# One set of expert blocks in place of two in a fused graph, attention and expert layer: 114 blocks, seven slots apart among the gathers

## The chip, the cores and the metric

The kernel runs on one core of a Trainium2 chip. The metric is the time of one execution on the device in microseconds (us), the median of several runs. The core has five engines with a queue of instructions each: PE (matmuls, with its weight loads shown as PEld), DVE (vector work, reads PSUM), ACT (activations and copies), POOL (here almost only indirect DMAs, which gather or scatter rows by a list of indices) and SP (issues the plain DMAs). Each queue runs in order and waits on semaphores for the others. Transfers between memory (HBM) and the on-chip SBUF run on 16 DMA engines.

## The reference

6250 nodes with 256 features, 100,000 edges, 16 experts, two experts a node:

```python
xn = layernorm(x)
# graph part, dinv = rsqrt(segment_sum(edge_weight, dst) + 1)
h   = xn @ W
agg = segment_sum((dinv[src] * edge_weight * dinv[dst])[:, None] * h[src], dst) + (dinv * dinv)[:, None] * h
g   = relu(0.5 * (layernorm(agg + b) * gamma + beta) + 0.5 * xn)
# linear attention, 8 heads of 32
q, k = elu(xn @ Wq.T) + 1, elu(xn @ Wk.T) + 1;  v = xn @ Wv.T
m   = ((q @ (k.T @ v)) / max(q @ k.sum(), 1e-6)) @ Wproj.T + bproj
x   = x + g + m
# experts
y   = layernorm(x)
top2, idx = top_k(y @ gate_w + gate_b, 2);  w = softmax(top2)
moe = sum over k of w[k] * (relu(y @ w1[idx[k]] + b1[idx[k]]) @ w2[idx[k]] + b2[idx[k]])
out = x + layernorm(y + moe) * f_gamma + f_beta
```

## The kernel before

Nodes lie in 49 tiles of 128 rows (the last has 106); `X` holds all of x in SBUF. Edges come sorted by destination, so each chunk of 128 edges adds into a window of two tiles. `gps_layer` tests this and takes `windowed_layer`. After the node degrees and the first norms, a loop over *slots* does everything that is left. A slot from 0 to 781 handles one chunk of 128 edges: POOL gathers the 128 source rows from `hs` (L1155), DVE builds the weighted one-hot matrix `hot` (L1159), and six slots later (`LAG`) PE multiplies both into the accumulator `acc` (L1168), which DVE adds into the tile's aggregate (L1177). All other work is woven in between: `weave.add(slot, piece)` registers a Python generator, the loop runs every piece that is due at a slot up to its next `yield n`, and puts it back n slots later. A slot is thus a place in the order of every engine's queue, not a time; PE, DVE, ACT and SP keep this order as it is written (`by_hand`). The slots go on behind 781, without gathers, until nothing is left.

The pieces that matter here:

- `residual(ts_)` finishes two tiles (graph norm, attention, relu), writes the new x and the gate's logits.
- `route(...)` runs for a *phase*, a group of tiles. It takes the top two experts of each token and gives each pair a row in `xslots`, a tensor in HBM of blocks of 128 rows, each block of one expert. An expert's last, part-filled block stays open (`fill`, `had`, `open`) and takes tokens of the next phase. Full blocks are put in a list in the order in which they become full (`queue` counts them, `code` holds them), and `listed` writes expert and block number of entries lo to hi into `rows`. Where `flush` is set, open blocks are closed too. `usual` goes to zero when a phase's list is shorter than the plan in the code needs (or longer, for a flush); then a second loop behind the first one runs every possible block and every combine once more.
- `scatter(...)` normalises the phase's tiles and POOL scatters their rows to `xslots` (L911), two DMAs a tile.
- `expert(...)` runs block j of the list. At its slot SP reads two registers from `rows`, asks for the first half of the expert's weights (512 KB) and for the block's 128 rows; 5 slots later for the second half (642 KB); at +9 PE transposes the rows (`xtp`, L973), at +11 it makes the hidden layer (`hp`, L983), at +13 the output (`yp`, L992), to which DVE adds the bias (L996); at +15 SP stores 128 rows to `yslots`. For the first blocks the steps are one slot shorter twice. Four weight buffers take turns.
- `token_weights` makes the two softmax weights; `combine(ts_)` gathers for two tiles their two rows each from `yslots` (POOL, L1019), adds them with the weights (DVE, L1030), normalises and writes `out`.

The blocks are in two sets with tensors, lists and states of their own: tiles 0 to 35 in eight phases, tiles 36 to 48 in three. Each set ends with a flush.

```python
SETS = ((8, 12, 16, 20, 24, 28, 32, 36), (42, 46, NT))
USUAL = [2 * CUT + 11, 2 * (NT - CUT) + 12]        # 83 and 38 blocks are run
hi = USUAL[z] if flush else max(0, 2 * (b - CUT * z) - 11)
block = max(block + (4 if z else 8 if n < 3 else 5 if flush else 6), ready)
```

So blocks start every 8, 6 and 5 slots in the first set and every 4 in the second, and not before their phase's routing is ready. Combines of tiles 0 to 35 may start 18 slots after the start of the first set's last block, those of the other tiles 18 slots after the start of the last block. One combine (two tiles) starts every 5 slots, and none before the last `residual` is 24 slots old. `fill` writes zeros into `xslots` and `yslots` ahead of their use, a megabyte at a time.

Of the kernel before, what the change touches and what calls it, by code (L numbers as in the profile page):

```python
# [117 lines left out]
SETS = ((8, 12, 16, 20, 24, 28, 32, 36), (42, 46, NT))  # L118
CUT = SETS[0][-1]
USUAL = [2 * CUT + 11, 2 * (NT - CUT) + 12]  # L120
MOST = [(2 * n + NE * (P - 1)) // P for n in (CUT * P, N - CUT * P)]

# [114 lines left out]
def windowed_layer(ctx: ExitStack, tc: tile.TileContext, X, rows3, ident, loc_t, w_t, W, b, gamma, beta, wqT, wkvT, wprojT, bproj,  # L237
# [12 lines left out]
    xslots = [dram.tile([(m + 1) * P, D], F32, name=f"w_xslots{i}") for i, m in enumerate(MOST)]  # L250
    yslots = [dram.tile([(m + 1) * P, D], F32, name=f"w_yslots{i}") for i, m in enumerate(MOST)]
# [110 lines left out]
    def fill(z, a):  # L362

        zero = zero_b.bitcast(F32)
        for s in range(0, MOST[z] + 1, 8):
            q = min(8, MOST[z] + 1 - s)
            nc.sync.dma_start(a[s * P:(s + q) * P, :].rearrange("(p q) c -> p q c", q=q),
                              zero[:, None, :].to_broadcast([P, q, D]))
            yield 8

    for _ in fill(0, xslots[0]):
        pass
# [350 lines left out]

    states = [state(f"s{z}") for z in range(len(SETS))]

# [27 lines left out]
    def listed(s, ps_row, lo, hi, most, closed):  # L753


        code = mp.tile([1, P], I32, name="code_i", bufs=1)[:, lo:hi]
        v.tensor_tensor(code, ps_row[0:1, lo:hi], iota_row[0:1, lo:hi], op=OP.add)
        v.tensor_scalar(s["rows"][:, 1, lo:hi], code, 8, None, op0=OP.logical_shift_right)
        v.tensor_scalar(s["rows"][:, 1, lo:hi], s["rows"][:, 1, lo:hi], float(NE - 1), float(P), op0=OP.min, op1=OP.mult)
        v.tensor_scalar(code, code, 255, None, op0=OP.bitwise_and)  # L760
        if not closed:
            past = small("past", P)[0:1, lo:hi]
            v.tensor_scalar(past, iota_row[0:1, lo:hi], s["queue"][0:1, :], 256.0, op0=OP.is_ge, op1=OP.mult)
            v.tensor_tensor(code, code, past, op=OP.add)
        v.tensor_scalar(s["rows"][:, 0, lo:hi], code, float(most), float(P), op0=OP.min, op1=OP.mult)

    def route(z, a, b, lo, hi, fresh, flush):
# [3 lines left out]
        s = states[z]  # L771
# [40 lines left out]
        if flush:  # L812
            done = small("done")
            v.tensor_copy(done, new)
        if not fresh:
# [60 lines left out]
        if hi > lo:  # L876
            row = bank("row")
            nc.tensor.matmul(row[0:1, :P], s["code"], ident, start=True, stop=True)
            listed(s, row, lo, hi, MOST[z], flush)
        v.scalar_tensor_tensor(usual, s["queue"][0:1, :], float(hi), usual,  # L880
                               op0=OP.is_le if flush else OP.is_ge, op1=OP.mult)

        if not flush:
            yield 1
            v.tensor_copy(s["last"], d[:, NE * m:])
# [7 lines left out]
    def scatter(z, n, a, b, ahead, kind, each):  # L893
# [13 lines left out]
        for t in range(a, b):  # L907
            r = rows(t)
            y = places[t]()
            for k in range(2):  # L910
                i = nc.gpsimd.indirect_dma_start(  # L911
                    out=xslots[z], out_offset=IndirectOffsetOnAxis(ap=slot_i[:r, t, k:k + 1], axis=0),
                    in_=y[:r], in_offset=None).ins
                for m in range(n + 1):
                    tc.declare_no_dep(i, group=f"tokens{z}_{m}", reason="every token has slots of its own")
                tc.declare_no_dep(i, group=f"loads{z}", reason="blocks that are read are full")
                tc.add_to_no_dep_group(f"tokens{z}_{n}", i)
# [24 lines left out]
    def expert(z, n, j, homes, bank, gap):  # L942

        def row(i):
            if not loaded.get((z, i)):
                _, regs = nc.values_load_multi_w_load_instructions(
                    states[z]["rows"][0:1, i, j:min(j // 8 * 8 + 8, ends[z, j])], engines=[mybir.EngineType.SP],
                    min_val=0, max_val=(MOST[z] if i == 0 else NE - 1) * P,
                    skip_runtime_bounds_check_because="bounded by a minimum where it is computed")
                loaded[z, i] = list(regs)  # L950
            return loaded[z, i].pop(0)
# [7 lines left out]
        i = sync(xs, xslots[z][bass.ds(slots, P), :])  # L959
        if n is not None:  # L960
            for m in range(n + 1, len(SETS[z])):
                tc.declare_no_dep(i, group=f"tokens{z}_{m}", reason="a full block takes no more tokens")
            tc.add_to_no_dep_group(f"loads{z}", i)
# [36 lines left out]
        i = sync(yslots[z][bass.ds(slots, P), :], y)  # L1000
        if n is not None:
            tc.declare_no_dep(i, group=f"stores{z}", reason="every block has rows of its own", keep=[before_it])
            tc.add_to_no_dep_group(f"stores{z}", i)
        homes["y"].give(y_)

    def combine(ts_, homes, pool, last):
# [7 lines left out]
        for i, t in enumerate(ts_):  # L1014
            r = rows(t)
            z = 0 if t < CUT else 1
            for k in range(2):
                got[i, k] = homes["got"].take()
                nc.gpsimd.indirect_dma_start(  # L1019
                    out=got[i, k]()[:r], out_offset=None, in_=yslots[z],  # L1020
                    in_offset=IndirectOffsetOnAxis(ap=slot_i[:r, t, k:k + 1], axis=0))
# [68 lines left out]
    to_fill = [(0, yslots[0]), (1, xslots[1]), (1, yslots[1])]  # L1090
    fill_at = 4
    for z, a in to_fill:
        weave.add(fill_at, fill(z, a))
        fill_at += 8 * ((MOST[z] + 8) // 8)
# [6 lines left out]
    a = 0  # L1101
    for z, phases in enumerate(SETS):
        lo = 0
        for n, b in enumerate(phases):
            flush = n == len(phases) - 1
            for t0 in range(a, b, 2):
                t1 = min(b, t0 + 2)
                at = max(at, min(NCH, 16 * t1 + 4) + LAG + 3)
                weave.add(at, residual(range(t0, t1)))
                last_at = at  # L1110
                for t in range(t0, t1):
                    summed_at[t] = at + 3
                    if t + RING < NT and t >= 4:
                        sum_from(t + RING)
                at += 10
            hi = USUAL[z] if flush else max(0, 2 * (b - CUT * z) - 11)
            ready = max(last_at + RES, scattered - 2)
            weave.add(ready, route(z, a, b, lo, hi, n == 0, flush))
            if flush:
                weave.add(ready + 6, token_weights(CUT * z, b))  # L1120
            slow = 0 if z and flush else 1
            weave.add(ready + 2, scatter(z, n, a, b, 9, "token" if slow else "got", slow))
            scattered = ready + 11 + 2 * (b - a) * slow
            ready += 14 + (2 * (b - a) * slow)
            for j in range(lo, hi):
                ends[z, j] = hi
                block = max(block + (4 if z else 8 if n < 3 else 5 if flush else 6), ready)
                weave.add(block, expert(z, n, j, homes, bank, (4, 3) if n < 3 and z == 0 else (5, 4)))
            lo, a = hi, b
        if z == 0:  # L1130
            ready_a = block + 18
# [56 lines left out]
    with tc.If(again), ExitStack() as tail:  # L1188
# [16 lines left out]
        for z, s in enumerate(states):  # L1205
            row = bank("row")
            nc.tensor.matmul(row[0:1, :P], s["code"], ident, start=True, stop=True)
            listed(s, row, 0, MOST[z], MOST[z], True)
            for j in range(MOST[z]):
                ends[z, j] = MOST[z]  # L1210
                weave.add(block, expert(z, None, j, homes, bank, (5, 4)))
                block += 4
# [493 lines left out]
```

## Time and profile before

| | |
|---|---|
| runs | 1540.73, 1544.71, 1543.6 us; median 1543.6 |
| profiled execution | 1551.48 us, of which the span shown is 1549.6 |
| busy share of the span | PE 83%, PEld 66%, DVE 59%, ACT 34%, POOL 62% |
| mean granted PE clock | 0.932 |
| DMA | 367.43 MB, mean 237 GB/s |
| chain that ended last | PE 41%, DVE 16%, DMA 12%, issue 10%, ACT 3% |
| expert blocks | 121 transfers each of `xslots` blocks, `yslots` blocks and both weight halves |

The page shows one profiled execution, which took some 8 us longer than the median run. The busy share is a mean over stages that have different limits. In a row of a group, the columns are line, engine, operation, out<-in and count, then busy time and mean ns of one, then the engine's idle time just before these instructions and what ended most of it. In order of time, a row is start, duration, engine, line, operation and, in brackets, the idle time before it and what ended it.

### The profile page before, as it was taken

What the parts mean: (1) busy time and instruction counts of PE and PEld (TensorE: products, weight loads), DVE (VectorE), ACT (ScalarE), POOL (GpSimd) and SP (SyncE); (2) the same over time, 40 slices, a digit from 0 to 9 for tenths busy, and PEclk for the clock granted to TensorE, in tenths of its full rate; (3) what the DMA queues carried; (4) which work ended last, traced back from release to release, by engine and by line L of the source; (5) the groups of instructions that cost most, each with busy time, mean ns of one, the idle gap of its engine ahead of it and who ended that gap; (6) DMA issues with size and microseconds to landing.
All of it is one profiled execution on the core that took longest, in us unless ns stands there. A gap on an engine that the chain in (4) does not pass through costs nothing.

```text
span 1549.6 us, 24825 instructions
## 1 busy us (share of the span) xinstructions
PE 1282.6 (83%) x7112; PEld 1017.6 (66%) x7112; DVE 918.8 (59%) x3246; ACT 519.5 (34%) x1388; POOL 965.7 (62%) x999
## 2 busy tenths in 40 slices
PE   4879999989767989898999989889999987777820
PEld 3836666666545767677787778768877865666620
DVE  7754444468855755646465475754573737788045
ACT  3654444423221323223232323323332334344220
POOL 1027777777777777777777777777677545551042
PEclk9999999999878999999999989989999999799975
DMA  9789933333345766768887868678888866999832
GB/s 288 250 288 378 356 104 99 99 99 117 101 166 182 230 219 233 238 221 276 277 281 259 278 234 295 210 237 301 316 292 301 299 245 225 327 360 326 313 95 68
DMA packets 180847, 367.43 MB, mean 237 GB/s; under 512 B 27091, under 2 KB 118152, under 8 KB 180694
## 3 DMA queue, kind: packets, MB, share of 16 engines
q1 hardware_dynamic: 132746, 236.69, 43.9%
q0 software_dynamic: 47712, 128.17, 25.9%
q8 instruction: 63, 1.03, 0.3%
q10 hardware_dynamic: 236, 0.80, 0.2%
q14 instruction: 90, 0.74, 0.2%
HBM read 290.00 MB, written 75.54 MB: 236 GB/s over the span
## 4 chain that ended last, share of the span: by engine, by line
PE 41%; DVE 16%; DMA 12%; issue 10%; ACT 3%; POOL 1%; SPq 0%; ACTq 0%; POOLq 0%; DVEq 0%
PE acc L1168 12%; PE yp L992 9%; DMA rows<-w_hs,src_t 8%; PE hp L983 8%; PE hp L667 3%; PE mix L683 2%; DMA early<-in_experts 2%; DVE hot L1159 2%; PE kq L549 2%; DMA w_xslots<-Q,slot_i 1%; DVE xn L1030 1%; DVE bnst L312 1%; DVE agg L1177 1%; PE tp L638 1%; PE gl L710 1%
## 5 line engine op out<-in xcount | busy, mean ns | idle before, releaser
L1155 POOL DMA_INDIRECT rows<-w_hs,src_t x782 | 758.1, 969 | 335.5 <-issue 91.1
L1168 PE MATMUL acc<-rows,hot 128*128 128x256 f32 x1564 | 447.3, 399 | 59.0 <-DMA rows<-w_hs,src_t 48.9
L1168 PEld LDWEIGHTS acc<-rows,hot 128*128 128x128 f32 x1564 | 276.9, 196 | 125.3 <-issue 51.1
L1159 DVE TENSOR_SCALAR hot<-iota_g,loc_t,w_t 128x128 f32<-128x128 f32 x782 | 244.9, 352 | 6.0 <-PE acc L1168 5.4
L1019 POOL DMA_INDIRECT Q<-w_yslots,slot_i x98 | 99.4, 1015 | 167.0 <-issue 90.2
L992 PE MATMUL yp<-early,hT 128*128 128x256 f32 x592 | 152.1, 403 | 24.0 <-ACT hT L988 24.0
L983 PE MATMUL hp<-Q,early 128*128 128x128 f32 x1184 | 150.4, 282 | 10.1 <-ACT Q L977 10.1
L983 PEld LDWEIGHTS hp<-Q,early 128*128 128x128 f32 x1184 | 146.5, 197 | 17.9 <-ACT Q L977 14.5
L992 PEld LDWEIGHTS yp<-early,hT 128*128 128x128 f32 x592 | 116.9, 201 | 46.2 <-ACT hT L988 29.3
L988 ACT ACTIVATE hT<-hp,early 128x128 f32<-128x128 f32 x296 | 84.3, 367 | 178.2 <-PE hp L983 108.1
L911 POOL DMA_INDIRECT w_xslots<-Q,slot_i x98 | 102.3, 1044 | 43.1 <-issue 32.0
L977 ACT COPY Q<-xtp 128x256 f32<-128x256 f32 x121 | 44.8, 370 | 232.6 <-PE xtp L973 226.2
L1177 DVE SCALAR_TENSOR_TENSOR agg<-acc,dinv,agg 64x256 f32<-64x256 f32 x135 | 65.1, 482 | 94.4 <-PE acc L1168 91.9
L983 PE MATMUL hp<-Q 128*128 128x128 f32 x752 | 101.1, 292 | 12.8 <-ACT Q L977 12.7
L983 PEld LDWEIGHTS hp<-Q 128*128 128x128 f32 x752 | 96.7, 205 | 20.1 <-ACT Q L977 18.7
L996 DVE TENSOR_TENSOR Q<-yp,early 128x256 f32<-128x256 f32 x74 | 31.2, 422 | 125.6 <-PE yp L992 124.4
L992 PE MATMUL yp<-Q,hT 128*128 128x256 f32 x376 | 92.8, 390 | 9.6 <-ACT hT L988 9.6
L549 PE MATMUL kq<-early,xnT 128*128 128x512 f32 (+1 forms) x196 | 96.6, 616 | 4.4 <-ACT xnT L545 4.4
L555 DVE SCALAR_TENSOR_TENSOR row<-two_a,two_b 128x256 f32<-128x256 f32 (+1 forms) x49 | 21.0, 429 | 130.3 <-ACT two_b L553 130.3
L988 ACT ACTIVATE hT<-hp,Q 128x128 f32<-128x128 f32 x188 | 53.5, 367 | 99.4 <-PE hp L983 67.3
L992 PEld LDWEIGHTS yp<-Q,hT 128*128 128x128 f32 x376 | 70.9, 193 | 22.6 <-ACT hT L988 13.4
L996 DVE TENSOR_TENSOR Q<-yp,Q 128x256 f32<-128x256 f32 x47 | 19.9, 423 | 105.5 <-PE yp L992 102.9
(262 smaller groups left out, 1776.5 us busy)
## 6 DMA issues: line engine op xcount, KB each, us to landing
early<-in_experts SPq DMA_DIRECT2D x74, 642.0 KB
early<-in_experts SPq DMA_DIRECT2D x74, 512.0 KB
Q<-in_experts SPq DMA_DIRECT2D x47, 642.0 KB
Q<-in_experts SPq DMA_DIRECT2D x47, 512.0 KB
w_xslots<-zero_b SPq DMA_DIRECT2D x16, 1024.0 KB
w_yslots<-zero_b SPq DMA_DIRECT2D x16, 1024.0 KB
Q<-w_xslots SPq DMA_DIRECT2D x121, 128.0 KB
w_yslots<-Q SPq DMA_DIRECT2D x121, 128.0 KB
```

The lines of the kernel that those rows point to most:

```text
L549: nc.tensor.matmul(kq[:r], xnT[:, k, :r], wkq[:, k, :], start=(k == 0), stop=(k == 1))
L667: nc.tensor.matmul(hp[:r0, i, :], agT[:, k, i * P:i * P + r0], w_sb[:, k, :], start=(k == 0), stop=False)
L911: i = nc.gpsimd.indirect_dma_start(out=xslots[z], out_offset=IndirectOffsetOnAxis(ap=slot_i[:r, t, k:k + 1], axis=0), in_=y[:r], in_offset ...
L983: nc.tensor.matmul(hp[:, f, :], w1[:, c, f * P:(f + 1) * P], xT[:, c, :], start=(c == 0), stop=(c == 1))
L988: act(hT[:, f, :], hp[:, f, :], AF.Relu, bias=b1[:, f:f + 1], scale=1.0)
L992: nc.tensor.matmul(yp[:, :D], hT[:, f, :], w2[:, f, :], start=(f == 0), stop=(f == FJ - 1))
L996: v.tensor_add(y, yp[:, :D], b2)
L1019: nc.gpsimd.indirect_dma_start(out=got[i, k]()[:r], out_offset=None, in_=yslots[z], in_offset=IndirectOffsetOnAxis(ap=slot_i[:r, t, k:k + ...
L1155: nc.gpsimd.indirect_dma_start(out=hrows[c], out_offset=None, in_=hs, in_offset=IndirectOffsetOnAxis(ap=src_t[:, c:c + 1], axis=0))
L1159: v.tensor_scalar(hots[c], iota_g[:, group_of(c) % 2, :], loc_t[:, c:c + 1], w_t[:, c:c + 1], op0=OP.is_equal, op1=OP.mult)
L1168: nc.tensor.matmul(accs[g], hots.pop(c), hrows.pop(c), start=begin, stop=end)
L1177: v.scalar_tensor_tensor(agg(t)[p0:p1], acc[p0:p1, :], dinv[p0:p1, t:t + 1], agg(t)[p0:p1], op0=OP.mult, op1=OP.add)
```

## The change

There is one set of blocks. Phases end at tiles 8, 12, ... 36, 40, 46 and 49. In the phase that ends at tile 40 (`part`, index `AFTER`), the blocks that are open from before and that got no 128th row are closed and listed together with the full ones, as long as at most 15 of the 16 experts are concerned; blocks begun with tokens of tiles 36 to 39 stay open. From then on tokens of tiles 0 to 35 lie only in the first 85 blocks of the list (`FIRST`); `usual` is also cleared when there are more. Only the last phase flushes. 114 blocks are run in place of 121. They start every 7 slots up to the phase of tile 40, then every 4. Combines of tiles 0 to 35 wait for the store of block 84 by a dependency set by hand, and start 18 slots after that block; later stores are declared independent of these gathers. `xslots` and `yslots` are one tensor each; the first 88 blocks of `xslots` are filled at the start, the rest in the loop behind `yslots`.

```diff
-SETS = ((8, 12, 16, 20, 24, 28, 32, 36), (42, 46, NT))
-CUT = SETS[0][-1]
-USUAL = [2 * CUT + 11, 2 * (NT - CUT) + 12]
-MOST = [(2 * n + NE * (P - 1)) // P for n in (CUT * P, N - CUT * P)]
+PHASES = (8, 12, 16, 20, 24, 28, 32, 36, 40, 46, NT)
+CUT = 36
+AFTER = PHASES.index(CUT) + 1
+FIRST, USUAL = 2 * PHASES[AFTER] + 5, 2 * NT + 16
+MOST = P
...
+        if part:
+            old = small("old")
+            v.scalar_tensor_tensor(old, whole, 0.0, s["had"], op0=OP.is_equal, op1=OP.mult)
+            few = small("few", 1)
+            v.tensor_reduce(few, old, axis=AX.X, op=OP.add)
+            v.tensor_scalar(few, few, NE - 0.5, None, op0=OP.is_lt)
+            v.tensor_tensor(old[:, NE - 1:], old[:, NE - 1:], few, op=OP.mult)
+            v.tensor_tensor(usual, usual, few[0:1, :], op=OP.mult)
+            done = small("done")
+            v.tensor_tensor(done, whole, old, op=OP.add)
...
+        if part:
+            v.scalar_tensor_tensor(usual, s["queue"][0:1, :], float(FIRST), usual, op0=OP.is_le, op1=OP.mult)
...
+            if part:
+                v.tensor_scalar(old, old, -1.0, 1.0, op0=OP.mult, op1=OP.add)
+                v.tensor_tensor(some, some, old, op=OP.mult)
+                v.tensor_tensor(left_i, left_i, old, op=OP.mult)
...
+            stores[j] = i
+            if j >= FIRST:
+                tc.declare_no_dep(i, group="gathers", reason="later blocks hold no token of the first tiles")
+                tc.add_to_no_dep_group("late", i)
...
+                if t < CUT and FIRST - 1 in stores:
+                    tc.declare_no_dep(g, group="late", reason="later blocks hold no token of the first tiles")
+                    tc.add_manual_dep(g, stores[FIRST - 1].name, ...)
+                    tc.add_to_no_dep_group("gathers", g)
...
-    to_fill = [(0, yslots[0]), (1, xslots[1]), (1, yslots[1])]
+    for a, first in (yslots, 0), (xslots, SOON):
+        weave.add(fill_at, fill(a, first, MOST + 1))
...
-            hi = USUAL[z] if flush else max(0, 2 * (b - CUT * z) - 11)
+        hi = USUAL if flush else 2 * b - (9 if n < AFTER else -1 if n == AFTER else 4)
...
-            if flush:
-                weave.add(ready + 6, token_weights(CUT * z, b))
+        if flush or n == AFTER:
+            weave.add(ready + 6, token_weights(*((CUT, NT) if flush else (0, CUT))))
...
-                block = max(block + (4 if z else 8 if n < 3 else 5 if flush else 6), ready)
-                weave.add(block, expert(z, n, j, homes, bank, (4, 3) if n < 3 and z == 0 else (5, 4)))
-        if z == 0:
-            ready_a = block + 18
+            block = max(block + (7 if n <= AFTER else 4), ready)
+            weave.add(block, expert(n, j, homes, bank, (4, 3) if n < 3 else (5, 4)))
+            if j == FIRST - 1:
+                ready_a = block + 18
```

## The prediction

> **What bounds the kernel now.** I read the page first (busy shares, costliest groups), then the table of stretches, then the order of time on POOL and PE where stretches differ, and the chain of waits for the last third.
>
> ```profile
> span 1549.6 us, 24825 instructions
> PE 1282.6 (83%) x7112; PEld 1017.6 (66%) x7112; DVE 918.8 (59%) x3246; ACT 519.5 (34%) x1388; POOL 965.7 (62%) x999
> L1155 POOL DMA_INDIRECT rows<-w_hs,src_t x782 | 758.1, 969 | 335.5 <-issue 91.1
> ```
>
> PE is busiest, so seven blocks fewer look like seven blocks' time. The stretches say otherwise (columns: busy us and count of PE, PEld, DVE, ACT, POOL; then PE clock, DMA share, GB/s):
>
> ```profile
> 420.00:520.00 100.00, 73.40 (x325) 56.29 (x326) 57.99 (x234) 23.90 (x58) 76.54 (x78) 0.81 0.52 176
> 920.00:1020.00 100.00, 91.67 (x496) 75.84 (x495) 61.11 (x214) 31.37 (x82) 76.25 (x78) 0.95 0.69 232
> 1100.00:1224.00 124.00, 119.37 (x713) 103.20 (x712) 70.79 (x249) 41.32 (x119) 91.63 (x95) 1.00 0.86 294
> 1250.00:1330.00 80.00, 57.74 (x306) 47.52 (x305) 47.17 (x169) 30.42 (x84) 38.65 (x38) 0.87 0.78 272
> 1330.00:1445.00 115.00, 90.98 (x522) 76.10 (x521) 86.54 (x238) 45.25 (x138) 41.03 (x40) 0.94 0.94 334
> 1445.00:1487.00 42.00, 33.25 (x203) 27.71 (x201) 3.41 (x10) 13.67 (x43) 0.00 (x0) 1.00 0.61 210
> 1487.00:1550.00 63.00, 0.00 (x0) 0.00 (x0) 37.52 (x104) 6.49 (x16) 26.89 (x26) 0.53 0.30 86
> ```
>
> Up to 1224 us POOL issues 77 to 79 row gathers and scatters per 100 us whether PE is busy 73 or 92 of them. In order of time POOL is back to back, one per 1.25 us (0.95 and a pause of 0.30), broken only in a few places by PE (the first two lines) and then behind the last edge gather:
>
> ```profile
> 1104.71 0.95 POOL L1155 DMA_INDIRECT rows<-w_hs,src_t  x1 [1.16 <-PE acc L1168]
> 1106.93 0.94 POOL L1155 DMA_INDIRECT rows<-w_hs,src_t  x1 [1.27 <-PE acc L1168]
> ...
> 1223.52 0.95 POOL L1155 DMA_INDIRECT rows<-w_hs,src_t  x1 [0.30 <-PE hp L983]
> 1236.54 1.00 POOL L911 DMA_INDIRECT w_xslots<-Q,slot_i  x1 [12.07 <-issue]
> 1253.21 0.99 POOL L1019 DMA_INDIRECT Q<-w_yslots,slot_i  x1 [6.50 <-DMA w_yslots<-Q]
> 1287.48 1.07 POOL L1019 DMA_INDIRECT Q<-w_yslots,slot_i  x1 [20.70 <-DVE xn L1030]
> 1297.12 1.00 POOL L911 DMA_INDIRECT w_xslots<-Q,slot_i  x1 [1.66 <-ACT xn L1023]
> ```
>
> So three stages: a POOL-bound one to 1224 us; a tail to 1486, in which PE runs the remaining blocks; and 63 us in which the last 13 tiles are combined behind the last block's store. In the tail the pure pace of a block is 5.29 us (hp of one block to hp of the next), with two short ACT waits in it; the chain shows where it is lost, and after such a loss the same eight matmuls take 3.78 instead of 2.00:
>
> ```profile
> 1454.92 2.05 PE L983 MATMUL hp<-Q 128*128 128x128 f32 x16 [0.52 <-ACT Q L977]
> 1457.48 2.00 PE L992 MATMUL yp<-Q,hT 128*128 128x256 f32 x8 [0.51 <-ACT hT L988]
> 1459.32 0.38 PE L973 MATMUL xtp<-ident,Q 128*128 128x128 f32 x2
> 1460.21 2.05 PE L983 MATMUL hp<-Q,early 128*128 128x128 f32 x16 [0.52 <-ACT Q L977]
> 1324.07 3.78 PE L992 MATMUL yp<-early,hT 128*128 128x256 f32 x8 [4.85 <-ACT hT L988]
> ```
>
> ```profile
> 1257.96 7.45 DMA early<-in_experts
> 1315.08 8.47 DMA early<-in_experts
> ```
>
> **The change part by part.**
>
> *Seven blocks go, and where.* A block is on PE 16 hp (2.05 us), 8 yp (2.00) and 2 xtp (0.38): 4.4 us, so 31 us of PE for seven. Stepping through the loop's arithmetic gives each block's slot; its yp falls 11 or 13 slots later. The last edge's matmuls stand at slot 787. Before, 82 of 121 blocks have their yp by slot 788: 39 are left. After, at one per 7 slots, 75 of 114 have it by slot 789: 39 are left. So all seven come out of the POOL-bound stage, and the tail keeps its 39. Worth of the seven there: (a) POOL's own losses to PE, the waits above 0.30 us between 1099 and 1135, sum to about 3.5 us[...]; I take 4 us (0 to 6). (b) PE's backlog: the last gather is issued at 1223.5, its acc matmul runs at 1236, 12.7 us later[...]. With one block per 7 slots instead of 5 in the last 150 slots (7 x 1.25 = 8.75 us for 4.4 us of block and 7 x 0.57 = 4.0 us of acc, by 447.3 us over 782 edges) PE is still full when residuals come, but not behind for long: I take 7 us (3 to 10). Together 11.
>
> *The tail's order.* From the DVE adds behind yp (L996), block 82 of before starts at 1242.4 and the last at 1485.95: 243.5 us for 39 blocks, against 39 x 5.29 = 206.3. The 37.2 us lost lie, by the distances of these adds, 11.4 at the last residual tiles and the first block of the second set (its wait for weights, 7.45 above), 8.6 beside the last route and the first gathers, 13.1 behind the last route (2.7 us for rows, 4.85 for weights, then yp at 3.78), and some 4 beside the rest of the combines. Before, the two late phases start blocks at the very slot in which their routing is ready (795 and 829): SP reads the row number there, so weights cannot be asked for earlier, and the last scatters (slot 817) stand in POOL's queue behind gathers of slot 815 that wait 20.70 us for DVE to free their buffers. After, the block counter is behind, not the routing: the phase of tiles 40 to 45 is ready at slot 799 and used at 822, the last one is ready at 829 and used at 850, and the first gather comes at slot 852, behind all scatters. I keep 8 us for the residuals' PE work and 4 for the routes. 25 blocks then run beside combines at before's pace there: from 1336.9 to 1407.4 twelve blocks, 5.87 us each, 0.58 over the pure pace: 14.5. Sum 26.5 to 27 lost instead of 37.2: **10 us less** (2 to 20).
>
> *Combines of the first 36 tiles* move from slots 815-902 to 852-937: 72 gathers on POOL, 36 output transfers in SP's queue among weight loads, and DVE's seven operations a tile. The density (5 slots for two tiles, 4 for a block) is unchanged, so DMA share there stays near 0.94; that is in the 5.87. The last early combine is written at slot 952, the last block's yp at 963: eleven slots, some 15 us, of the 68 us of slack that before has between its last early gather (1407) and the last store.
>
> *The new wait* of the early gathers is for the store of block 84 (slot 849), right ahead of the first gather at 852. Behind it on POOL stand only other gathers; nothing but DVE's combines waits for them. I take nothing: 39 minus 10 blocks run meanwhile.
>
> *Added DVE work* in one route: ten operations of 0.17 us (L802's kind), 1.7 us, at slots 677-692 where DVE is busy 60 of 100 us and POOL sets the pace: nothing; uncovered, 1.7. The state has seven memsets fewer. *Fills*: the same 34 transfers of zeros up to 1 MB, all by slot 190, ahead of the first y store; DMA share is 0.34 then: nothing. *SP*: 28 DMAs fewer, none added. *Pitch 7 for 8* at the first 21 blocks, then 7 for 6: at slot 600 both have started 50 or 51 blocks: nothing; were POOL's cover gone, one block's 4.4 us. *End*: the last 13 tiles hang on the last store as before, 63 us.
>
> [...] In the rows, PE's clock falls to 0.81 in 420-520, where PE is busy 73 of 100 us, and to 0.87 in 1250-1330, where it waits. [...] POOL issues 78 at clock 0.81 as at 0.95, so the slower matmuls are hidden. [...] The rows beside combines are at 0.94 with weight waits that stay, so I follow the rows.
>
> **Sum.** 4 + 7 + 10 = 21 us off the profiled 1551.5 (span 1549.6): 1530.5. The median shown is 1543.6, 7.9 under the profiled execution; the same 21 us off it is 1522.6, so **1523**.
>
> **The rivals.**
> *Hidden anyway*: PE's backlog at slot 787 stays (residuals cause it), and the tail's waits come back later as weight loads beside denser DMA (0.94 to 1.00 already). For it: PE at 119 of 124 us before 1224. Against: the pure stretch 1445-1487 has DMA at 0.61 to spare. It leaves the 4 us: 1540, 1534 to 1546.
> *Early combines become the last thing*: they end 11 slots ahead of the last block; on POOL the final 26 gathers queue behind them. Before, 72 gathers take 154 us (1253 to 1407), with 20.70 us of it one wait. After they can start near 1296; up to 1450 nothing is lost. It ends slower than before from the point where they take over 190 us (2.6 us a gather instead of 2.14); at 2.75 it is 8 to 10 us slower: 1553. For it: each gather waits on DVE xn. Against: the 20.70 was for a jam with routing that is gone.
> *The flag fails*: the block list must have 81 blocks closed at tile 40, and counting the reference's routing on its inputs gives 81, no margin (111 real blocks in all, before 116). A token that swaps experts would run all 128 blocks again: 128 x 5.29 + 98 x 1.25 and some 30 us, about 830 more. Only one token of 6250 has its second and third logit within 1e-5.
> *More than that*: all waits and half-rate windows go: 28 to 38 off.
>
> **How the numbers follow.** Forecast 0.72 (its own range 1508 to 1536), hidden anyway 0.12, combines last 0.09, flag 0.01, more 0.06. 0.3% is 4.6 us, about what a measurement of this kernel can tell from no change. Faster: 0.72 + 0.06 + 0.05 of hidden anyway = 0.83; same 0.07; slower 0.10. The range takes the forecast, most of "more" and the near half of "hidden anyway": 1506 to 1541.
>
> **What would show it.** POOL still at 77 to 79 per 100 us, its last edge gather at 1217 to 1223; the acc behind it within 6 us; 39 blocks left then; no PE wait above 2 us between 1250 and 1320; the last L996 add near 1465; 63 us behind it. Wrong if POOL's rate rises (PE was the bound), if early gathers end after the last store, or if weight waits above 4 us fill the combine stretch.

## The result and the profile after

The changed kernel takes 1528.81 us (median of four runs, 1524.69 to 1530.15); the kernel before took 1544.15 beside it (four runs, 1540.73 to 1545.44). The ratio is 0.9897, with an interval of 0.988 to 0.9913: 15.3 us less, where 21 were forecast. The profiled execution of after took 1528.39, of before 1551.48, so the two traces differ by 23.1 us. The profiled execution of before lay 7.3 us above the median of its four runs, that of after 0.4 below: the difference of 7.7 us belongs to these executions, and not to the change. In two of the four jobs below the kernel before itself took 1789 to 1809 us, for a reason that no trace shows, so of those only ratios inside a job are read.

The page of after, busy time by engine and the gathers of the edges:

```profile
span 1526.6 us, 24293 instructions
PE 1252.2 (82%) x6930; PEld 981.7 (64%) x6930; DVE 921.1 (60%) x3262; ACT 509.3 (33%) x1353; POOL 967.0 (63%) x999
L1181 POOL DMA_INDIRECT rows<-w_hs,src_t x782 | 758.1, 969 | 333.0 <-issue 100.0
```

PE has lost 182 matmuls (7 blocks of 26) and 30 us of busy time, twice what the kernel gained. POOL has its 999 instructions and its 758.1 us of gathers unchanged. The table of stretches of after (columns as in the prediction: busy us and count of PE, PEld, DVE, ACT, POOL; PE clock, DMA share, GB/s), cut where after's stages end:

```profile
420.00:520.00 100.00, 74.67 (x344) 56.75 (x343) 59.33 (x233) 24.81 (x62) 76.22 (x79) 0.83 0.57 184
920.00:1020.00 100.00, 88.23 (x496) 72.53 (x494) 60.46 (x224) 29.45 (x82) 76.24 (x79) 1.00 0.76 252
1100.00:1219.00 119.00, 110.13 (x609) 91.26 (x609) 66.52 (x217) 35.80 (x97) 88.41 (x92) 0.97 0.78 260
1250.00:1310.00 60.00, 47.02 (x274) 38.80 (x274) 18.27 (x87) 19.41 (x59) 8.76 (x8) 0.94 0.76 264
1330.00:1445.00 115.00, 88.84 (x544) 74.57 (x543) 103.10 (x287) 50.45 (x152) 55.95 (x55) 1.00 0.99 357
1445.00:1462.00 17.00, 12.81 (x79) 10.76 (x79) 2.12 (x5) 4.57 (x17) 0.00 (x0) 1.00 0.62 225
1462.00:1527.00 65.00, 1.27 (x6) 0.76 (x5) 38.00 (x107) 8.43 (x20) 26.99 (x26) 0.55 0.29 83
```

The first three lines show POOL still at 77 to 79 per 100 us, with PE in the third now at 110 of 119 instead of 119 of 124: the seven blocks left the stage that POOL sets. The fifth line is new: DVE is busy 103 of 115 us beside the combines (86.5 before), DMA at 0.99. The last two lines are the end as it was.

POOL in order of time (start, duration, line, and the idle time ahead with what ended it), and below it PE:

```profile
1215.68 0.95 POOL L1181 DMA_INDIRECT rows<-w_hs,src_t  x1 [0.30 <-issue]
1229.58 1.00 POOL L931 DMA_INDIRECT w_xslots<-Q,slot_i  x1 [12.95 <-issue]
...
1284.25 1.56 POOL L931 DMA_INDIRECT w_xslots<-Q,slot_i  x1 [0.30 <-issue]
...
1307.94 0.99 POOL L1044 DMA_INDIRECT Q<-w_yslots,slot_i  x1 [20.27 <-DMA w_yslots<-Q]
```

```profile
1216.19 0.61 PE L795 MATMUL tots<-cnt,ones 128*128 128x16 f32 x2 [2.60 <-DVE cnt L786]
...
1218.06 3.62 PE L1005 MATMUL hp<-Q 128*128 128x128 f32 x16
...
1272.24 3.78 PE L1014 MATMUL yp<-Q,hT 128*128 128x256 f32 x8 [0.51 <-ACT hT L1010]
```

The last edge gather is at 1215.7 instead of 1223.5. All scatters (L931) now lie ahead of the first early combine gather (L1044), which waits 20.27 us for a store of `yslots`; no scatter stands behind it. PE's largest waits between 1250 and 1320 have shrunk to one of 2.4 us, for a count of the routing:

```profile
PE hp L1005 <- ACT Q L999: 6.1, 10, 1.5
...
PE tots L795 <- DVE cnt L786: 2.4, 1, 2.4
```

(Columns: us in total, times, longest.) The landmarks of the traces, read from single rows:

| | before | before, second execution | after |
|---|---|---|---|
| edge gathers, first to last | 1117.5 | 1122.0 | 1107.5 |
| last `acc` matmul behind the last gather | 12.7 | 12.6 | 11.4 |
| last `acc` matmul to last block's add | 249.8 | 242.7 | 236 |
| of that, combine stretch (first combine add, L1030 or L1059, to those of the 35th of the 36 early tiles) | 138.7 | 135.2 | 124.3 |
| last block's add to the end of the span | 63.7 | 62.7 | 63.3 |

The rows do not add up to the difference of the spans by themselves, because the first gather also starts 2.2 us later in after (108.2 instead of 106.0 us). The shortening of the tail shows in the combine stretch. Here it is in both kernels, before first, from the table of stretches:

```profile
1286.00:1425.00 139.00, 104.21 (x572) 86.84 (x570) 113.36 (x341) 55.28 (x161) 69.16 (x67) 0.90 0.88 312
```

```profile
1315.00:1439.00 124.00, 95.87 (x588) 80.62 (x588) 105.14 (x292) 55.52 (x164) 67.29 (x67) 1.00 1.00 365
```

PE's count is about the same, 572 and 588 matmuls, but DVE has 49 operations and 8.2 us less to do. Before, 48 operations of the last routing and its softmax weights (9.9 us of DVE) lay in this stretch; after, none do. DVE's idle time there went from 25.6 to 18.9 us.

### The profile page after: what moved, and what is told of

It reads as the page before. It is cut to its first block, busy times and chain, and to the rows that moved or that the text cites. A ratio compares the mean times of both kernels' runs of the same rounds, so it can differ in the third digit from the quotient of the medians.

```text
span 1526.6 us, 24293 instructions
## 1 busy us (share of the span) xinstructions
PE 1252.2 (82%) x6930; PEld 981.7 (64%) x6930; DVE 921.1 (60%) x3262; ACT 509.3 (33%) x1353; POOL 967.0 (63%) x999
## 4 chain that ended last, share of the span: by engine, by line
PE 39%; DVE 19%; DMA 15%; issue 5%; ACT 3%; POOL 2%; SPq 0%; ACTq 0%; POOLq 0%; DVEq 0%
PE acc L1194 12%; DMA rows<-w_hs,src_t 9%; PE yp L1014 9%; PE hp L1005 7%; DMA w_xslots<-Q,slot_i 3%; PE hp L671 2%; DVE xn L1059 2%; DVE hot L1185 2%; PE kq L553 2%; DVE bnst L315 2%; PE mix L687 2%; DMA Q<-in_experts 1%; DMA early<-in_experts 1%; POOL w_xslots L931 1%; PE gl L714 1%
## 5 line engine op out<-in xcount | busy, mean ns | idle before, releaser
L1181 POOL DMA_INDIRECT rows<-w_hs,src_t x782 | 758.1, 969 | 333.0 <-issue 100.0
L1185 DVE TENSOR_SCALAR hot<-iota_g,loc_t,w_t 128x128 f32<-128x128 f32 x782 | 247.1, 359 | 14.5 <-PE acc L1194 13.7
L1044 POOL DMA_INDIRECT Q<-w_yslots,slot_i x98 | 99.8, 1019 | 113.4 <-DMA w_yslots<-Q 64.4
L1005 PE MATMUL hp<-Q,early 128*128 128x128 f32 x1136 | 143.8, 281 | 12.5 <-ACT Q L999 12.2
L1005 PEld LDWEIGHTS hp<-Q,early 128*128 128x128 f32 x1136 | 139.6, 196 | 21.4 <-ACT Q L999 18.4
L931 POOL DMA_INDIRECT w_xslots<-Q,slot_i x98 | 103.2, 1053 | 75.6 <-issue 66.8
L1014 PE MATMUL yp<-early,hT 128*128 128x256 f32 x568 | 140.1, 390 | 12.8 <-ACT hT L1010 12.8
L1014 PEld LDWEIGHTS yp<-early,hT 128*128 128x128 f32 x568 | 107.8, 193 | 32.8 <-ACT hT L1010 18.4
L1018 DVE TENSOR_TENSOR Q<-yp,early 128x256 f32<-128x256 f32 x71 | 30.1, 424 | 122.6 <-PE yp L1014 122.6
L1005 PE MATMUL hp<-Q 128*128 128x128 f32 x688 | 88.2, 283 | 12.8 <-ACT Q L999 12.8
L1005 PEld LDWEIGHTS hp<-Q 128*128 128x128 f32 x688 | 84.0, 196 | 19.0 <-ACT Q L999 17.8
L1014 PE MATMUL yp<-Q,hT 128*128 128x256 f32 x344 | 85.2, 391 | 13.2 <-ACT hT L1010 13.2
L1010 ACT ACTIVATE hT<-hp,Q 128x128 f32<-128x128 f32 x172 | 49.1, 368 | 99.0 <-PE hp L1005 53.8
L1014 PEld LDWEIGHTS yp<-Q,hT 128*128 128x128 f32 x344 | 64.7, 193 | 25.8 <-ACT hT L1010 17.6
L321 ACT ACTIVATE sd<-mv,eps_t 128x2 f32<-128x2 f32 (+2 forms) x76 | 22.8, 300 | 152.7 <-DVE mv L316 148.7
```

Of the source, the lines that this page charges most:

```text
L931: i = nc.gpsimd.indirect_dma_start(out=xslots, out_offset=IndirectOffsetOnAxis(ap=slot_i[:r, t, k:k + 1], axis=0), in_=y[:r], in_offset=No ...
L1005: nc.tensor.matmul(hp[:, f, :], w1[:, c, f * P:(f + 1) * P], xT[:, c, :], start=(c == 0), stop=(c == 1))
L1010: act(hT[:, f, :], hp[:, f, :], AF.Relu, bias=b1[:, f:f + 1], scale=1.0)
L1014: nc.tensor.matmul(yp[:, :D], hT[:, f, :], w2[:, f, :], start=(f == 0), stop=(f == FJ - 1))
L1044: g = nc.gpsimd.indirect_dma_start(out=got[i, k]()[:r], out_offset=None, in_=yslots, in_offset=IndirectOffsetOnAxis(ap=slot_i[:r, t, k:k + ...
L1181: nc.gpsimd.indirect_dma_start(out=hrows[c], out_offset=None, in_=hs, in_offset=IndirectOffsetOnAxis(ap=src_t[:, c:c + 1], axis=0))
```

## The experiments

Two theories were set against each other for each part: that of the prediction (POOL sets the pace of the gather stage, PE's row of blocks that of the tail), and rivals (PE sets both; DVE or DMA sets the tail).

**b_look: the kernel before, profiled a second time.** No edit.

> The kernel before, unchanged, for a second profiled execution. The first profiled one took 1551.5 us, 7.9 over the median of its runs, that of the changed kernel 1528.4, its median. Theory: the edge-gather stage repeats within 2 us (last edge gather at 1223.5), and the 8 us lie in the tail, in the half-clock matmuls behind the weight wait near 1315; this look should then show the last block's DVE add near 1478 to 1481, and the last route's stall shorter. Rival: the tail repeats (last add near 1486) and the 8 us are in the start or the edge-gather stage.

1549.08 us, 5.2 over the median of the 51 runs of its job (1543.88; 1537.93 to 1554.09). The last block's add was at 1484.6, so the expected 1478 to 1481 was missed. Neither theory holds as it stands: the gather stage did not repeat within 2 us but was 4.5 us longer, and the tail was 7.1 us shorter. What a profiled execution of before has over the median does not sit in one stall.

**b_skip_gather: before, without blocks 56 to 63 of the first set.** These run wholly in the gather stage.

```diff
-                weave.add(block, expert(z, n, j, ...))
+                if (z, j // 8) != (0, 7):
+                    weave.add(block, expert(z, n, j, ...))
```

> The kernel before without the blocks 56 to 63 of the first set (slots 650 to 685), whose tokens then get no expert output: eight blocks fewer in the stage of the edge gathers, all other slots as they were. Theory (POOL sets that stage's pace): only POOL's waits for PE go, 3 to 9 us less. Rival (PE is the bound): 8 x 4.4 us of PE = 35 us less.

1542.33 us (12 runs), ratio 0.9986 (0.9966 to 1.0005): 1.5 us less for eight blocks, or nothing. PE as the bound of this stage (35 us) is excluded. POOL's theory is right in kind; of its 3 to 9 us less only the low end lies inside the measured interval (5.2 us less to 0.8 more). The stretch in which the blocks are missing, in this kernel and in before:

```profile
1010.00:1075.00 65.00, 55.51 (x255) 43.04 (x253) 39.23 (x118) 16.18 (x38) 49.73 (x51) 0.91 0.66 222
```

```profile
1010.00:1075.00 65.00, 60.03 (x327) 50.02 (x327) 35.66 (x109) 19.95 (x52) 49.74 (x51) 0.95 0.80 272
```

72 matmuls fewer, and POOL issues 51 with or without them, in the same busy time (49.73 and 49.74 us).

**b_skip_tail: before, without blocks 16 to 23 of the second set.** These run beside the combines.

```diff
+                if (z, j // 8) != (1, 2):
+                    weave.add(block, expert(z, n, j, ...))
```

> The kernel before without the blocks 16 to 23 of the second set (slots 857 to 885), whose tokens then get no expert output: eight blocks fewer behind the edge gathers, beside the early combines. Theory (the row of blocks on PE sets the tail's pace): 8 x 5.3 to 5.9 us = 42 to 47 us less. Rival (the early combines or the DMA engines set it): 8 x 4 us of weight transfer or less, under 32.

1541.22 us (20 runs), 0.9975 (0.9961 to 0.9989): 2.7 us less for eight blocks. That PE's blocks set this stretch (42 to 47 us) fell. The adds of the last block ahead of the hole and of the first one behind it, in this kernel and in before (L996, in order of time):

```profile
1362.89 0.42 DVE L996 TENSOR_TENSOR Q<-yp,early 128x256 f32<-128x256 f32 x1
1411.84 0.40 DVE L996 TENSOR_TENSOR Q<-yp,Q 128x256 f32<-128x256 f32 x1
```

```profile
1365.62 0.42 DVE L996 TENSOR_TENSOR Q<-yp,early 128x256 f32<-128x256 f32 x1 [1.34 <-PE yp L992]
1418.89 0.42 DVE L996 TENSOR_TENSOR Q<-yp,Q 128x256 f32<-128x256 f32 x1
```

The hole is 48.9 us long without the eight blocks and 53.3 us with them. The table of stretches inside it:

```profile
1363.00:1411.00 48.00, 7.22 (x33) 6.07 (x34) 42.48 (x118) 11.42 (x29) 23.18 (x23) 0.57 0.59 184
```

PE is busy 7 of 48 us and DMA at 0.59, but DVE 42.5: the combines go through DVE at 6.52 us for two tiles and hold the next block behind them in the order of the queues. With blocks between them two tiles take 7.06 us in before (mean of ten), 6.71 in its second execution and 6.94 in after (mean of 16). A block every 4 slots and a combine every 5 make 1.25 blocks for two tiles; their adds of 0.42 us put on the 6.52 give 7.05. So in before DVE sets this stretch. PE stands close behind: 1.25 blocks at the pure pace of 5.29 us would take it 6.61.

**b_late_combine: before, with the early combines 18 slots later.**

```diff
-    at = max(ready_a, last_at + RES)
+    at = max(ready_a, last_at + RES) + 18
```

> The kernel before with only the start of the combines of tiles 0 to 35 (and with it every later start among them) moved 18 slots back, from slot 815 to 833, behind the last scatters (slots 817 to 826). Theory of the jam (early gathers stand ahead of the last scatters on POOL and of the last routing on DVE): 4 to 9 us less, POOL's wait of 20.7 us and the weight wait of 8.5 us gone. Rival (the tail loses its time because the late phases' blocks start at the very slot of their routing): within 3 us of no change.

1542.77 us (22 runs), 0.9992 (0.9976 to 1.0008): no difference, so the jam theory (4 to 9 us) fell. The execution that was profiled took 1552.09, 9.3 us above this median. Its rows show that the edit did only a part of what was meant. POOL's queue is not among those that keep the written order, and eleven of the early gathers still stand ahead of the last six scatters (fifteen in before):

```profile
1269.75 0.94 POOL L1019 DMA_INDIRECT Q<-w_yslots,slot_i  x1 [0.30 <-PE hp L983]
1296.42 1.00 POOL L911 DMA_INDIRECT w_xslots<-Q,slot_i  x1 [25.72 <-issue]
```

The gathers' waits for DVE ahead of these scatters (20.70 and 3.34 us) are gone, and the scatters start 56.3 us behind the last `acc` instead of 61.0 (52.1 in after). The combine stretch shortens to 132.2 us, but starts later, and the last add is at 1486.6. Two block adds are still 12.9 us apart where the second phase of the second set begins. So taking DVE's part of the jam away gained nothing; all scatters ahead of all early gathers, as the changed kernel has them, was not tried in before.

**a_pitch6: the changed kernel with a block every 6 slots among the gathers.** In the jobs with the longer times, twice.

```diff
-            block = max(block + (7 if n <= AFTER else 4), ready)
+            block = max(block + (6 if n <= AFTER else 4), ready)
```

> The changed kernel with blocks 6 slots apart among the gathers, not 7. By slot 799 it has the yp of 77 or 78 blocks and not 75, but blocks 81 and 88 then start 6 and 4 slots behind the slot in which their routing is ready, not 23 and 21. Theory (the slack behind the two late routings is what the change gains in the tail): the waits for weights behind them come back, 5 us or more each, and eat most of the 3 x 5.29 = 16 us that the three blocks are worth: within 8 us of the changed kernel. Rival (the slack is worth nothing, only the count of blocks left counts): 12 to 16 us under it, near 1514.

> Blocks 6 slots apart among the gathers, once more, because in its first job the kernel before itself took 1808.6 us in place of 1544 (every engine's waits longer). If that was the surroundings, the kernel before is near 1544 here. Theory (slack behind the two late routings is what the change gains in the tail): within 8 us of the changed kernel's 1528.8. Rival (only the count of blocks left behind the gathers counts): 12 to 16 us under it, near 1514; the first job's ratio to the kernel before, 0.989, is that of the changed kernel (0.990) and speaks for the first.

Ratios to before 0.9893 (0.9831 to 0.9955) and 0.9949 (0.9927 to 0.9971). The changed kernel has 0.9897 in its own job and was not run in these, so the first tells nothing apart. The second speaks mildly against six slots, but this kernel took 1779.95 us there (1787.83 in the first job), where the changed one took 1528.81 in its own job. In a_skip_pure, from the first of the two jobs, POOL issues 62 per 100 us between 420 and 520 us instead of 79, so POOL's pace in these jobs is hardly the one of which the prediction speaks.

**a_skip_pure: the changed kernel without blocks 81 to 87; a_skip_combine: without blocks 96 to 103; a_no_add: without the last addition of x for tiles below 36.**

```diff
+            if not 81 <= j < 88:
+                weave.add(block, expert(n, j, ...))
```

```diff
+            if not 96 <= j < 104:
+                weave.add(block, expert(n, j, ...))
```

```diff
-            o = pool.tile([P, D], F32, name="row", bufs=3)
-            v.tensor_add(o[:r], y[:r], X[:r, t, :])
-            sync(out[t * P:t * P + r, :], o[:r])
+            o = pool.tile([P, D], F32, name="row", bufs=3) if t >= CUT else None
+            if t < CUT:
+                sync(out[t * P:t * P + r, :], y[:r])
+            else:
+                v.tensor_add(o[:r], y[:r], X[:r, t, :])
+                sync(out[t * P:t * P + r, :], o[:r])
```

> The changed kernel without the seven blocks 81 to 87 (slots 822 to 846, behind the edge gathers and ahead of the first combine), whose tokens then get no expert output. Theory (in this stretch the row of blocks on PE sets the pace): 7 x 5.29 = 37 us under the changed kernel, near 1492. Rival (something beside the blocks, the last routing or DVE, sets it): under 15 us.

> The changed kernel without blocks 81 to 87 (slots 822 to 846, between the edge gathers and the first combine; their tokens get no expert output), once more for the same reason. Theory (in this stretch PE's row of blocks sets the pace): 7 x 5.29 = 37 us under the changed kernel, near 1492. Rival (the last routing, DVE or something else sets it): under 15 us.

> The changed kernel without the eight blocks 96 to 103 (slots 882 to 910, beside the combines of the first 36 tiles), whose tokens then get no expert output. Theory, new after the skip in the tail of the kernel before (2.7 us for eight blocks): DVE sets the pace beside combines, some 6.5 us for two tiles without a block and 0.43 a block: 3 to 8 us under the changed kernel, near 1523. Theory of the prediction (PE's row of blocks at 5.87 us): 47 us. Rival (DMA engines, busy 0.99 there): 8 x 4 us of transfer = 32 us.

> The changed kernel without the last addition of x in the combines of tiles 0 to 35 (one DVE operation of 0.42 us a tile), whose output lacks that x. DVE theory: 36 x 0.42 = 15 us under the changed kernel, as long as nothing else comes first. DMA theory (0.99 busy, 357 GB/s beside the combines): under 4 us, since the bytes stay. Between these: DVE goes first and DMA stands close behind.

All three were slower than before in these jobs: 1.0341 (1.0273 to 1.0409) and again 1.036 (1.0299 to 1.042), 1.012 (1.0061 to 1.018), 1.0191 (1.0124 to 1.0258). The changed kernel itself was not run beside them. No theory had less work taking longer. The table of stretches of a_skip_pure, in a part that is the same as in the changed kernel:

```profile
420.00:520.00 100.00, 71.34 (x278) 49.59 (x276) 66.31 (x236) 26.51 (x57) 62.38 (x62) 0.80 0.31 94
```

POOL issues 62 per 100 us instead of 79 and DMA moves half: POOL is no longer back to back, the premise of every estimate here. These four runs say nothing of the changed kernel at 1529 us, and what made them slow stays open.

**a_pool_add: the changed kernel with the last addition of the early combines on POOL instead of DVE.** If DVE sets the stretch, this should help.

```diff
-            v.tensor_add(o[:r], y[:r], X[:r, t, :])
+            (nc.gpsimd if t < CUT else v).tensor_add(o[:r], y[:r], X[:r, t, :])
```

> The changed kernel with the last addition of x in the combines of tiles 0 to 35 done by POOL and not by DVE; nothing is left out. DVE theory (DVE is back to back beside the combines, some 6.5 us for two tiles): 36 x 0.42 = 15 us under the changed kernel, as far as nothing else comes first; since the DMA engines are 0.99 busy there, 3 to 10 us, near 1521. DMA theory: within 3 us of it. POOL theory (its additions hold up the gathers queued behind them): slower.

1534.75 us (9 runs), ratio 0.9938 (0.9913 to 0.9963), in a job in which before took 1544.43. The changed kernel had 0.9897 in its own job: some 6 us were lost, with intervals that just meet (0.988 to 0.9913 there). Groups of instructions by line (columns: count, busy us, mean ns, idle us ahead), first from after, then from this kernel, both between 1331 and 1452 us:

```profile
L1059 DVE SCALAR_TENSOR_TENSOR xn<-Q,w,xn 128x256 f32<-128x256 f32 x65 | 31.3, 481 | 1.2
L1068 DVE SCALAR_TENSOR_TENSOR xn<-xn,rs,par 128x256 f32<-128x256 f32 x34 | 16.5, 486 | 1.2
```

```profile
L1059 DVE SCALAR_TENSOR_TENSOR xn<-Q,w,xn 128x256 f32<-128x256 f32 x63 | 43.2, 686 | 1.1
L1068 DVE SCALAR_TENSOR_TENSOR xn<-xn,rs,par 128x256 f32<-128x256 f32 x33 | 17.7, 537 | 1.2
L315 DVE BATCH_NORM_STATS2 bnst<-xn 128x6 f32<-128x256 f32 x32 | 13.7, 428 | 1.1
...
L1070 POOL TENSOR_TENSOR row<-xn,X 128x256 f32<-128x256 f32 x35 | 28.5, 815 | 26.3 <-DVE xn L1068 16.8 <-issue 7.5 <-POOL row L1070 1.8
```

DVE is rid of 35 additions of 425 ns, 14.9 us. But its own operations are slower while POOL adds: 63 of L1059 by 205 ns and 33 of L1068 by 51 (537 against 486) give back 14.6 us. DVE was busy 101 of these 121 us, in after 103, and POOL's gathers now stand behind adds that wait for DVE. The combine stretch took 130.2 us instead of 124.3. The run does not relieve DVE, so it does not show that DVE sets this stretch in the changed kernel too, how much is to be had there, or whether PE's blocks or DMA, at 0.97, would be next.

**a_pool_add6: the same with a block every 6 slots among the gathers.** The prediction's count of blocks in the tail against the slack behind the late routings.

```diff
-            block = max(block + (7 if n <= AFTER else 4), ready)
+            block = max(block + (6 if n <= AFTER else 4), ready)
```

> The same, and blocks 6 slots apart among the gathers, not 7. Count theory: 36 or 37 blocks are left behind the gathers and not 39, 12 to 16 us under the kernel with the additions on POOL alone. Slack theory (blocks again start 4 to 6 slots behind their routing, so the waits for weights return): within 8 us of it.

1538.51 us (20 runs), 0.9959 (0.9945 to 0.9973), by the medians 3.8 us more than a_pool_add in the same job, with intervals that overlap. The number is the one of the slack theory, and the 12 to 16 us less of the count did not come. But the trace gives the count little to count: behind the last `acc` lie 39 block adds, against 40 in a_pool_add, so one block left the tail and not two or three. The chain of waits of this kernel behind the late routings:

```profile
1269.73 6.83 DMA early<-in_experts
...
1277.08 3.78 PE yp L1014 x8
...
1282.51 3.16 DMA Q<-w_xslots
...
1286.10 3.78 PE yp L1014 x8
```

The blocks have caught up with the routing again: PE waits for weights that were asked for late, then for rows, and the next eight matmuls take 3.78 us each time, as behind the waits of before. The waits that the change removed are back, by this one digit. Yet the loss does not show in the tail, which is 2 to 3 us shorter than in a_pool_add (some 242 us from the last `acc` to the last add). It shows among the edge gathers: the last one starts at 1221.9 instead of 1215.5, and the 782 gathers were busy 8.4 us longer. Their groups in a_pool_add and in this kernel:

```profile
L1181 POOL DMA_INDIRECT rows<-w_hs,src_t x782 | 757.9, 969 | 333.3 <-issue 97.5
L1181 POOL DMA_INDIRECT rows<-w_hs,src_t x782 | 766.3, 980 | 333.6 <-DMA w_yslots<-zero_b 90.8
```

Two executions of before differ by 4.4 us in the same sum (758.1 and 762.5), so one trace does not tell whether the denser blocks cause it. The run shows that the waits return with less slack; what they cost it does not show. None of these kernels beats the changed one.

## Why the prediction was right, and where its steps were off

**The seven blocks in the gather stage.** Right: they were worth little more than the waits they caused POOL. Eight blocks taken from that stage gave 1.5 us, and POOL's pace in the traces did not move. The added DVE operations, the fills and the pitch at the first blocks cost nothing that shows.

**Step (a), POOL's own losses, −4.** The waits above 0.30 us fell from 9.9 to 4.6 us over the whole stage, −5.3 (12.9 in the second profile of before). But the stage shortened by 10.0. What the prediction overlooked: with a phase ending at tile 40 instead of 42, four scatters fewer stand ahead of the last edge gather (80 instead of 84), and at 1.29 us each, in the queue that sets this stage, that is 5.2 us. The prediction had moved the phase's blocks and not the phase's DMAs. The 5.2 us are counted from the traces; no run moved the scatters alone. The gathers themselves gained nothing by fewer weight loads: beside eight blocks' loads in before and without them in b_skip_gather, 51 of POOL's DMAs have the same busy time (49.74 and 49.73 us).

**Step (b), PE's backlog behind the last gather, −7.** It was −1.3, below the lower bound of 3; the last `acc` still runs 11.4 us behind the gather, and the sign "within 6 us" failed. Not all of that distance is backlog: where the chain of before last goes through the landing of gathered rows, at 1158.6, 1171.2 and 1177.5 us, they landed 4.79, 6.04 and 6.78 us after their issue. The backlog itself did shrink. The routing of the phase that ends at tile 46 puts two small matmuls (`tots`) into PE's queue here. In before they came late and waited for nothing:

```profile
1226.75 0.29 PE L792 MATMUL tots<-cnt,ones 128*128 128x16 f32 x2
...
1228.06 1.95 PE L983 MATMUL hp<-Q,early 128*128 128x128 f32 x16
```

That is 3.2 us behind the start of the last gather. In after PE was free for them at 1213.6, 2.1 us ahead of it, waited 2.60 us for DVE's count, and ran the next hp in 3.62 us instead of 1.95 (the granted clock was 0.66 between 1215 and 1225 us). These 4.3 us are most of what is missing of the 7. So the time that the blocks freed on PE was taken by a wait for DVE and the slower hp behind it, for which the prediction had no term. The rival "hidden anyway" had the small size right, though it gave the residuals as the cause.

Together the two steps came to −11.3 in the traces for a forecast of −11. That is luck: one was 6 us too small and the other 6 us too large.

**The tail, −10.** In size about right: −13.5 between the profiles (−6.7 against the second profile of before), the last add at 1463.3 for a forecast of 1465. In the prediction's own terms, from the distances of the block adds: the seven blocks up to 1287.9 lost 12.7 us against the pure pace of 5.29, where 8 + 4 were forecast. The 32 blocks behind lost 6.1 in all, where the stretch beside the combines alone was put at 14.5. That makes 18.8 us lost instead of 26.5; but the first of these adds now comes 11.1 us behind the last `acc` instead of 6.2. The mis-sized term is the pace beside the combines. The two adds at the ends of 25 blocks there in after:

```profile
1314.35 0.42 DVE L1018 TENSOR_TENSOR Q<-yp,early 128x256 f32<-128x256 f32 x1 [4.85 <-PE yp L1014]
1452.73 0.42 DVE L1018 TENSOR_TENSOR Q<-yp,Q 128x256 f32<-128x256 f32 x1 [5.98 <-PE yp L1014]
```

That is 5.54 us a block instead of 5.87. The 5.87 came from one execution of before; in the second one the same twelve blocks took 5.58 each, so most of this difference is not the change's.

The premise of the term was wrong too: it priced these blocks as PE's. b_skip_tail shows that eight of them are worth 2.7 us in before, where DVE's combines set the stretch. That they set it in after as well is argued from the same pace for two tiles, and not shown. The time between the last `acc` and the last add outside the combine stretch was about the same, 111 us before (107.5 in the second profile) and 112 after. So the gain shows inside it, 138.7 to 124.3: by the two stretches 8.2 us less work for DVE, mostly the last routing's, which now runs ahead of the combines where DVE is busy a third of the time (18 of 60 us between 1250 and 1310), and 6.7 us less idling of DVE. This is read from the traces; no run isolated it.

The waits for weights behind the late routings went, as forecast. PE's longest wait between 1250 and 1320 us is now the 2.4 for a count, which still breaks the sign "no wait above 2". With less slack the weight waits return (a_pool_add6), but what their absence is worth stays open. Changing only the phases was not tried on the chip.

**The clock.** At a granted clock of 1.00 the two rows of before at 0.87 and 0.94 would be some 17 us shorter, an estimate from 13% of 80 us and 6% of 115; the prediction kept to the rows and took 10 for the tail. In before the clock was 0.50 from 1324 to 1336 us, where yp and hp took 3.78 us each, behind the wait of 4.85 us; no run isolated what set it. The clock in the combine stretch did go from 0.90 to 1.00. The measured −13.5 lies between 10 and 17, and −6.7 against the second profile lies below both, so the traces do not decide between them. Where DVE sets the stretch, as in before (2.7 us for eight blocks in b_skip_tail), PE's rate there is not time saved.

**Early combines last.** Did not happen: the first gather waited 20.27 us for its store, and the last early tile's add (L1059) ended at 1442, 21 us before the last block's. The end was 63 us, as said.

**The sum against the median.** By profile −23.1, by median −15.3; 21 were forecast for both. The prediction took its base and its losses from one execution that lay 7.9 us above the median then known. The second lay 5.2 above its median, the profiled execution of after 0.4 below. Part of the losses counted in the trace of before were that execution's own. The pace beside the combines is one of them; for the rest two traces can't tell, since the excess lay in other places in each. Differences of a few us between single traces, as in the steps above, are to be read with this in mind.

## What to carry to other kernels

When work is taken from a stage, ask first which engine's pace the stage keeps, and count everything that the change moves in that engine's queue: here four scatters on POOL took 5.2 us of its queue by their rows, while eight expert blocks taken from PE gave 1.5 us. An engine that is freed early may only meet the next wait sooner, as PE met DVE's count (2.60 us). A stretch in which PE is busy 79% (91 of 115 us beside the combines in before) and often waits may still be set by another engine. Taking eight blocks out and finding the hole nearly as long (48.9 us instead of 53.3) showed that DVE's chain of small operations held the order. An edit of the order holds only for the queues that keep it: in b_late_combine POOL's did not take it over. Where the profiled execution lies above the median, expect the gain by the median to fall short of the sum of stalls counted in it.

## What the runs showed of the hardware

In a_pool_add, between 1331 and 1452 us, POOL made 35 additions of 815 ns each. Three DVE lines, each with two inputs in SBUF, took longer there than in the same window of after: L1059 686 ns instead of 481, L1068 537 instead of 486 and L1067 482 instead of 471. The statistics L315, with one input, stayed at 428, and the block adds L1018, whose one input lies in PSUM, at 424 (425 in after). The mean loss for one L1059 is 205 ns, and offloading an addition of 425 ns was worth nothing. What slows these lines, and whether it goes by their inputs, no run isolated.

In before and after most of POOL's gathers of the edges kept a period of 1.25 us (0.95 and a pause of 0.30) where nothing held them: in before between 420 and 520 us, at a mean PE clock of 0.81, as between 1100 and 1224 us, at 1.00. Equal executions of the kernel before spread over 16 us, from 1537.9 to 1554.1, in one job.
